# A third Strassen level in two more pairs of steps, index operations spread over six places, and a 26th buffer

## The chip, the cores and the metric

The kernel runs on one core of a Trainium2 chip. A core has five engines that run side by side, each in its own order: TensorE multiplies matrices (PE in the profile; its weight loads are PEld), VectorE (DVE), ScalarE (ACT) and GpSimd (POOL) work element by element, and SyncE (SP) here only issues DMA transfers. ScalarE and GpSimd issue transfers too. The metric is device time in microseconds (us); lower is better. Before the change it is 2588.83 us, the median of three runs (2587.49 to 2589.33).

## The reference, cut to what matters

```python
# x: (32, 128, 2048) float32; two layers, each x + ffn(cond(x))
def layer0(x):
    att = softmax(mlp(cond_128))                                  # (32, 8)
    agg_w = einsum('bk,koi->boi', att, weight)                    # a 128x128 matrix per batch
    y = einsum('boi,bih->boh', agg_w, x) + (att @ bias_k)[:, :, None]
    out = einsum('bsd,od->bso', y, W) + bias                      # 2048 x 2048
    xa = einsum('bsd,erd->ebsr', y, A)                            # 16 low-rank terms
    return x + out + einsum('ebsr,eor,e->bso', xa, Bf, coeffs * scales)

def layer1(x):
    y = grouped_conv_9_taps(x) + (cond_128 @ c_weight.T)[:, :, None] + fside
    t = y.reshape(4096, 2048)[:, perm].reshape(4096, 16, 128)
    t = gelu(einsum('bhd,hdm->bhm', t, up))                       # 16 heads, 128 -> 512
    t = einsum('bhm,hmd->bhd', t, down).reshape(4096, 2048)
    return x + t[:, argsort(perm)].reshape(32, 128, 2048)
```

The product with W is 4096 x 2048 x 2048, and it is the part that the change touches. The kernel folds the low-rank terms into W, multiplies x by that sum first, and applies the 128x128 mixing of each batch afterwards.

## The kernel before, in words

**The large product.** It is done by Strassen's method in Winograd's form, where seven products of halves take the place of eight. At the first level the seven products are the rounds P1, P2, P6, P7, P5, P3, P4 (`ROUNDS`). Each round has eight steps, g = 0 to 7; a step takes four batches, 512 rows of x. Step numbers below are these g, with the round's name; step i of the whole is 8 times the round's place plus g. Inside a step the second level is written out: `multiply` makes seven products, each of four matmuls of 128x512 into one PSUM bank, and VectorE (`add`) or, where the target is fresh, ScalarE adds or copies the bank into the accumulator in SBUF. The profile records two rows for each matmul instruction of the program, so four matmuls stand there as x8.

**The third level.** `PAIRS` names the pairs of neighbouring steps that use it: pair n is the steps 2n and 2n+1. In such a pair both steps go through `multiply_third`, which makes only the five products P1, P5, P6, P3, P7. The products P2 and P4 of both steps are together made as seven quarter products in the second step of the pair (`quarter`): each is four matmuls of 128x256, and one VectorE addition takes its bank into the accumulator. In the first round these stand after the step's five products, in P2 between them (`early`). The quarter products need three kinds of sums:
- the weights' quarters, once a round (`third_weights`): eight GpSimd subtractions of 128x256 (L393, L394, L399) and four VectorE subtractions (`quarter_ops`, L1130) in the gaps of the step;
- the x quarters, once a pair (`third_inputs`): four additions or subtractions of 128x512 (L419 to L422) from the x tiles of both steps, on the engine that the caller gives, put into a tile named `sq`;
- the accumulator of the first step, which is held until the second has ended (`held`); both are then stored.

**What runs beside it.** For each step GpSimd makes four sums of x (`x_combine`, L311 to L314), one step ahead. In the first round TensorE also makes the blocks of W with their low-rank terms (`w_make_two`, L223, at the top of steps 0 to 5); VectorE adds them to the loaded W (L226) and sums their rows (L243, L1140, L1141), and GpSimd stores them (L168). In P2 GpSimd forms the blocks of the next round (`outer_weights`, L283 with tile `wo_P`). Between the products VectorE makes the mixing matrices of the batches (`mixed_kernel`, L563, L565). Small preparations come from a generator, `small()`: `next(chain)` runs one piece of it at the end of a step, and from step i = 5 on two pieces. Its last piece computes the row numbers of the gathers and scatters of layer 1 on VectorE (L997 to L1005): thirteen operations on 128x16 integers.

**What sets the order.** The order of instructions on each engine is the order in which the program issues them (`manual_schedule`); the framework only adds semaphore waits. An engine works strictly in order, and a DMA queue issues strictly in order. SBUF tiles of 8 KB per partition come from one pool, `big`, with `SLOTS` buffers; a new tile takes over a buffer that was freed and waits for its last users. Eight PSUM banks go round.

**Layer 1** follows after the last round: mixing, convolution (`conv_begin`, `conv_middle`, `conv_end`, with three small tiles cq, cs, cr), then a gather, two matmuls with gelu between, and a scatter for each of 128 pairs of row group and head.

Of the kernel before, what the change touches and what calls it, by code (L numbers as in the profile page):

```python
# [8 lines left out]
FP = mybir.dt.float32  # L9
# [7 lines left out]
P = 128  # L17
B = 32
L = 2048
QW = 512  # L20
# [4 lines left out]
NPH = 4  # L25
# [6 lines left out]
GB = 4  # L32
NG = B // GB
GT = GB * P
SLOTS = 25

# [10 lines left out]


PAIRS = {
    "P1": (2, 3), "P2": (0, 1, 2), "P6": (0, 1, 2, 3), "P7": (0, 1, 2, 3),
    "P5": (0, 1, 2, 3), "P3": (0, 1, 2, 3), "P4": (0,),
}
ENDS = ("P1", "P4")
# [3 lines left out]
def adaln_ffn_kernel(  # L59
# [16 lines left out]
    nc = tc.nc  # L76

    dram = ctx.enter_context(tc.tile_pool(name="dram", bufs=1, space=DRAM))
    const = ctx.enter_context(tc.tile_pool(name="const", bufs=1))
    agp = ctx.enter_context(tc.tile_pool(name="agp", bufs=2))  # L80
    big = ctx.enter_context(tc.tile_pool(name="big", bufs=SLOTS))
    psum = ctx.enter_context(tc.tile_pool(name="psum", bufs=1, space=PSUM))
    banks = [psum.tile([P, QW], FP, name=f"bank{i}", tag=f"bank{i}") for i in range(8)]

    def slot(name, shape=(P, L)):
        return big.tile(list(shape), FP, name=name, tag="s")


    def bank():
        return banks.pop(0)  # L90

    def done(*ps):
        banks.extend(ps)
# [22 lines left out]
        for g in range(NG)  # L116
    }

    ident = const.tile([B, B], FP, name="ident", tag="ident")
    make_identity(nc, ident)  # L120
    mix = const.tile([P, KEXP, P], FP, name="mix", tag="mix")
    att_bc = const.tile([P, B * KEXP], FP, name="att_bc", tag="att_bc")
    aggb = const.tile([P, B], FP, name="aggb", tag="aggb")
# [6 lines left out]
    cs = const.tile([P, 4], FP, name="cs", tag="cs")  # L130
# [154 lines left out]
    def x_loads(r, g):  # L285
        return {
            "P1": lambda: [x_load(g, 0, 0)],
            "P2": lambda: [x_load(g, 0, 1)],
            "P6": lambda: [x_load(g, 1, 0), x_load(g, 1, 1), x_load(g, 0, 0)],
            "P7": lambda: [x_load(g, 0, 0), x_load(g, 1, 0)],  # L290
            "P5": lambda: [x_load(g, 1, 0), x_load(g, 1, 1)],
            "P4": lambda: [x_load(g, 1, 1)],
            "P3": lambda: [x_load(g, 0, 1), part_load("s2", g)],
        }[r]()

    def x_combine(r, g, ts):

        a = ts[0]
        tt = nc.gpsimd.tensor_tensor
        if r == "P6":  # L300

            b, a, c = ts
            pieces(b, b, a, ALU.add)
            pieces(a, b, c, ALU.subtract)
            part_store("s2", g, a)
        if r in ("P7", "P5", "P3"):
            pieces(a, a, ts[1], ALU.add if r == "P5" else ALU.subtract)
        xa[steps.index((r, g))] = a
        s = slot(f"s_{r}{g}", (P, 4, QW))
        a11, a12, a21, a22 = a[:, 0, 0], a[:, 1, 0], a[:, 0, 1], a[:, 1, 1]  # L310
        tt(s[:, 0], a21, a22, ALU.add)  # L311
        tt(s[:, 1], s[:, 0], a11, ALU.subtract)
        tt(s[:, 2], a11, a21, ALU.subtract)
        tt(s[:, 3], a12, s[:, 1], ALU.subtract)  # L314
        return {
            "P1": a11, "P2": a12, "P3": s[:, 3], "P4": a22,
            "P5": s[:, 0], "P6": s[:, 1], "P7": s[:, 2],
        }
# [90 lines left out]
    def in_pair(r, g):  # L409
        return g // 2 in PAIRS[r]  # L410

    def third_inputs(i, eng):

        (x11, x12), (x21, x22) = (
            [xa[n][:, 1, :, h * NQ : (h + 1) * NQ] for h in range(2)] for n in (i, i + 1)
        )
        tt = eng.tensor_tensor
        t = slot(f"sq_{i}", (P, 4, 2, NQ))
        tt(t[:, 0], x21, x22, ALU.add)  # L419
        tt(t[:, 1], t[:, 0], x11, ALU.subtract)  # L420
        tt(t[:, 2], x11, x21, ALU.subtract)
        tt(t[:, 3], x12, t[:, 1], ALU.subtract)  # L422
        return {
            "P1": x11, "P2": x12, "P3": t[:, 3], "P4": x22,
            "P5": t[:, 0], "P6": t[:, 1], "P7": t[:, 2],
        }
# [126 lines left out]
    late, ins, pms, xgs, x1ts, va, vb, hts, open_ = {}, {}, {}, {}, {}, {}, {}, {}, {}  # L553
# [135 lines left out]
    def conv_product(ps, k, i, v, first, last):  # L689

        for r, (out, rhs) in enumerate(zip(halves(ps), halves(v))):
            w = late["tw"][:, k - 1] if 1 <= k <= 4 else late["te"][:, k // 5]
            nc.tensor.matmul(  # L693
                out, lhsT=w[:, 2 * i + r], rhs=rhs,
                start=first and r == 0, stop=last and r == 1, skip_group_check=True,
            )

    def biased(out, ps, c, i, bias, scale):

        for r in range(2):  # L700
            for j in range(2):
                part = slice((2 * r + j) * NM, (2 * r + j + 1) * NM)
                b = 2 * c + j
                nc.scalar.activation(
                    out[:, part], ps[:, part], AF.Identity,
                    bias=bias[:, 2 * i + r, b : b + 1], scale=scale,
                )

    def conv_tile(c, i, name):
        return agp.tile([P, QW], FP, name=f"{name}_{c}{i}", tag=name, bufs=1)  # L710

    def conv_begin(c, i):
        px, py = bank(), bank()
        v = va[c, i]
        conv_product(px, 1, i, v[:, 0], True, False)
        conv_product(py, 3, i, v[:, 2], True, False)
        q, s = conv_tile(c, i, "cq"), conv_tile(c, i, "cs")
        biased(q, px, c, i, ctxb, 2.0)
        nc.scalar.mul(s, py, 2.0)
        open_[c, i] = px, py, q, s  # L720

    def conv_middle(c, i):
        px, py, q, s = open_[c, i]
        v = va[c, i]
        conv_product(px, 2, i, v[:, 1], False, False)
        conv_product(py, 4, i, v[:, 3], False, True)
        r = conv_tile(c, i, "cr")
        biased(r, py, c, i, ctxb, 2.0)
        nc.vector.tensor_tensor(q, q, px, ALU.subtract)
        nc.vector.tensor_tensor(s, s, py, ALU.subtract)  # L730

        nc.vector.tensor_tensor(v[:, 2], px, r, ALU.add)
        done(py)
        open_[c, i] = px, q, s, r
# [39 lines left out]
    def stage_second(c, n):  # L774
        if n in (6, 9):
            conv_middle(c, int(n == 9))
        if n in (5, 8):
            conv_inputs(c, int(n == 8), 1)
        if n in (0, 2):
            mix_begin(2 * c + n // 2)  # L780
# [5 lines left out]
    def third_products(c, n):  # L786
        if n in (5, 8):
            conv_begin(c, int(n == 8))
        if n in (6, 9):
            conv_end(c, int(n == 9))  # L790
        if n in (0, 2):
            mix_work(2 * c + n // 2)
# [71 lines left out]
        ws.append(t)  # L864

    def late_loads():
        late["tw"] = slot("tw_l", (P, 4, GR, P))
        nc.sync.dma_start(late["tw"].rearrange("p k r c -> p (k r c)"), tw_d)
        late["w1"] = slot("w1", (P, NPH, QW))
        nc.sync.dma_start(late["w1"].rearrange("p f n -> p (f n)"), w1_d.to_broadcast([P, L]))  # L870
        late["fb"] = slot("fb", (P, NPH, QW))
        nc.sync.dma_start(
            late["fb"].rearrange("p f n -> p (f n)"), fbias.to_broadcast([P, L])
        )


    def small():
# [3 lines left out]
        def take(rows, cols):  # L881
            used[0] += cols
            return sm[0:rows, used[0] - cols : used[0]]
# [8 lines left out]
        adiag = take(B, B * KEXP)  # L892
        ones = take(P, P)
        nc.gpsimd.memset(ones, 1.0)
        yield

        p0 = bank()
# [55 lines left out]
        for o in range(NPH):  # L953
# [44 lines left out]
        nc.vector.tensor_scalar(  # L998
            orow[:, 0], pos, 0x1FC, None, ALU.bitwise_and
        )  # L1000
        nc.vector.tensor_scalar(orow[:, 1], pos, 9, None, ALU.logical_shift_right)
        nc.vector.tensor_tensor(row, row, orow[:, 0], ALU.add)
        nc.vector.tensor_tensor(row, row, orow[:, 1], ALU.add)
        for g in range(NG):
            nc.vector.tensor_scalar(orow[:, g], pos, g * L, None, ALU.add)  # L1005
        yield


    ctx.enter_context(tc.manual_schedule())
# [44 lines left out]
    unsummed, unsummed_first = [], list(first)  # L1054
    olds = {}
    chain = small()
    nxt, waiting, ts, quarter_ops = {}, {}, {}, []
    heads = [(g, h) for g in range(NG) for h in range(NH)]
# [5 lines left out]
    for i, (r, g) in enumerate(steps):  # L1064
        ri = i // NG
        last_round = ri + 1 == len(ROUNDS)
        if i + 1 < len(steps):
            if i + 1 not in xs:
                xs[i + 1] = x_loads(*steps[i + 1])
            if not last_round:  # L1070
                lhs[i + 1] = x_combine(*steps[i + 1], xs.pop(i + 1))
                if g == 2 * PAIRS[r][0]:
                    quarters, quarter_ops = third_weights(r, rhs)
                if in_pair(r, g) and g % 2 == 0 and g > 0 and r != "P6":
                    sq = third_inputs(i, nc.gpsimd)
        if i == 0:
            olds_load(0)
        if i + 1 < len(steps) and not last_round and i != NG - 1:
# [31 lines left out]
        if last_round and g == 0:  # L1110
            quarters, quarter_ops = third_weights(r, rhs)
            late_loads()
# [49 lines left out]
        if in_pair(r, g) and g % 2 == 0 and (g == 0 or r == "P6" or last_round):  # L1162
            sq = third_inputs(i, nc.gpsimd if r in ENDS else nc.vector)
# [97 lines left out]
```

## Time and profile before

| what | value |
|---|---|
| median of three runs | 2588.83 us (2587.49 to 2589.33) |
| the profiled execution, its own time | 2590.78 us |
| its span (first to last instruction) | 2589.0 us |
| TensorE busy | 2574.6 us, 99% of the span |
| VectorE busy | 1514.5 us, 58% |
| GpSimd busy | 1362.8 us, 53% |
| ScalarE busy | 532.2 us, 21% |
| DMA, mean | 235 GB/s |
| mean granted TensorE clock | 0.999 |

The profile of one execution has a page with the busy time of each engine, its share in slices of the span, the DMA queues and the costliest groups of instructions. The trace behind it answers narrower questions: the waits (which instruction of an engine waited for which of another, total us, times, longest), the timeline (instructions in order of time: start, duration, engine, line, operation, output<-input, shape, count, and in brackets the idle time before it and what ended it), and the busy time by windows. Matmuls overlap, so a row's duration is longer than the distance to the next row; the distances of the starts are what they cost. Busy time says little about an engine that is not the last one waited for.

### The profile page before, as it was taken

To read this page: it belongs to the slowest core of one execution; us is meant where nothing else is said; L and a number is where in the kernel's file an instruction comes from. 1 tells how busy PE (TensorE), PEld (TensorE's weight loads), DVE (VectorE), ACT (ScalarE), POOL (GpSimd) and SP (SyncE) were. 2 spreads that over 40 slices of the span, in tenths; PEclk is the share of its full clock that TensorE was granted. 3 is DMA by queue.
4 is the path that set the end of the run, shared out by engine and by line. 5 is a ranking of instruction groups with operands and counts; after the bars stand their busy time and mean duration, and the time that the engine had idled before them with its cause. 6 is when DMAs were issued, how large, how long until landed. Compare 5 with 4: busy or idle time off the path is not lost. (4 is left out here: it accounts for less than half of the span.)

```text
span 2589.0 us, 21703 instructions
## 1 busy us (share of the span) xinstructions
PE 2574.6 (99%) x6998; PEld 1328.4 (51%) x6998; DVE 1514.5 (58%) x2368; ACT 532.2 (21%) x1099; POOL 1362.8 (53%) x1124
## 2 busy tenths in 40 slices
PE   9999999999999999999999999999999999999999
PEld 4445554455555555555554454455544454455543
DVE  5656565466555676654377666667666666666601
ACT  0000000000000000000011244444444444444432
POOL 7323756988977845977514234343444334434222
PEclk9999999999999999999999999999999999999999
DMA  7543467778467477573766887777767877787432
GB/s 324 210 163 129 162 235 317 289 296 336 187 246 296 189 316 297 199 317 156 254 229 228 256 303 254 241 243 232 228 225 234 258 232 222 226 257 234 161 127 89
DMA packets 186577, 608.30 MB, mean 235 GB/s; under 512 B 17632, under 2 KB 91872, under 8 KB 142304
## 3 DMA queue, kind: packets, MB, share of 16 engines
q1 hardware_dynamic: 147936, 473.48, 50.8%
q0 software_dynamic: 32704, 130.04, 15.0%
q10 hardware_dynamic: 5824, 3.40, 0.4%
q8 instruction: 56, 0.92, 0.1%
q14 instruction: 57, 0.47, 0.1%
HBM read 372.45 MB, written 200.84 MB: 221 GB/s over the span
## 5 line engine op out<-in xcount | busy, mean ns | idle before, releaser
L837 PE MATMUL bank<-t,ws 128*128 128x512 f32 x1024 | 460.3, 592 | 0.0
L848 PE MATMUL bank<-gl,ws 128*128 128x512 f32 x1024 | 460.2, 592 | 0.0
L855 POOL DMA_INDIRECT out<-t,orow x128 | 152.1, 1188 | 538.8 <-DVE t L853 478.6
L840 ACT ACTIVATE gl<-bank 128x512 f32<-128x512 f32 x512 | 305.8, 598 | 418.0 <-PE bank L837 415.4
L447 PE MATMUL bank<-P_t,s_P 128*128 128x512 f32 x704 | 314.5, 595 | 3.0 <-DVE p L440 3.0
L848 PEld LDWEIGHTS bank<-gl,ws 128*128 128x128 f32 x1024 | 194.6, 190 | 233.0 <-issue 231.5
L837 PEld LDWEIGHTS bank<-t,ws 128*128 128x128 f32 x1024 | 194.6, 190 | 226.6 <-issue 222.7
L586 POOL TENSOR_TENSOR x<-x,fb 128x512 f32<-128x512 f32 x128 | 177.1, 1412 | 227.5 <-DMA x<-in_x 159.5
L853 DVE TENSOR_TENSOR t<-bank,t 128x512 f32<-128x512 f32 x128 | 88.4, 690 | 325.0 <-PE bank L848 325.0
L440 DVE TENSOR_TENSOR u<-bank,u 128x512 f32<-128x512 f32 x204 | 134.0, 687 | 233.1 <-PE bank L447 214.1
L592 ACT ACTIVATE bank<-w,aggb 128x512 f32<-128x512 f32 x128 | 80.8, 684 | 867.3 <-DMA w<-w_d 855.0
L447 PE MATMUL bank<-wo_P,s_P 128*128 128x512 f32 x544 | 241.6, 592 | 0.0
L283 POOL TENSOR_TENSOR xt<-xt,xt 128x512 f32<-128x512 f32 x128 | 163.1, 1307 | 107.4 <-DMA xt<-in_xT 89.4
L447 PEld LDWEIGHTS bank<-P_t,s_P 128*128 128x128 f32 x704 | 134.3, 191 | 156.6 <-issue 152.7
L311 POOL TENSOR_TENSOR s_P<-xt 128x512 f32<-128x512 f32 x56 | 73.9, 1319 | 212.4 <-DMA xt<-in_xT 170.5
L565 DVE SCALAR_TENSOR_TENSOR ags<-mix,att_bc,ags 128x128 f32<-128x128 f32 x224 | 181.3, 810 | 4.7
L447 PEld LDWEIGHTS bank<-wo_P,s_P 128*128 128x128 f32 x544 | 103.4, 190 | 116.5 <-issue 113.6
L821 POOL DMA_INDIRECT t<-hx_d,row x128 | 131.2, 1025 | 57.0 <-issue 23.2
L440 DVE TENSOR_TENSOR p<-bank,p 128x512 f32<-128x512 f32 x84 | 56.6, 688 | 116.3 <-PE bank L447 111.6
L693 PE MATMUL bank<-va,tw_l 128*128 128x256 f32 x512 | 122.0, 380 | 2.2 <-DVE va L677 2.2
L447 PE MATMUL bank<-wo_P,xt 128*128 128x512 f32 x272 | 122.3, 592 | 0.0
L460 PE MATMUL bank<-P_q,sq 128*128 128x256 f32 x528 | 120.7, 379 | 0.4 <-DVE u L468 0.4
(191 smaller groups left out, 3515.8 us busy)
## 6 DMA issues: line engine op xcount, KB each, us to landing
xt<-in_xT SPq DMA_DIRECT2D x88, 1024.0 KB, 10.6
u<-u_d SPq DMA_DIRECT2D x40, 1024.0 KB, 10.2
wo_P<-wb_d SPq DMA_DIRECT2D x36, 1024.0 KB, 13.0
u<-c_d SPq DMA_DIRECT2D x64, 512.0 KB, 7.3
x<-in_x SPq DMA_DIRECT2D x32, 1024.0 KB, 9.3
xg<-x SPq DMA_DIRECT2D x256, 128.0 KB, 5.4
hx_d<-x1t SPq DMA_DIRECT2D x32, 1024.0 KB, 6.7
hx_d<-ht SPq DMA_DIRECT2D x32, 1024.0 KB, 4.8
```

The costliest lines, as they stand in the source:

```text
L283: nc.gpsimd.tensor_tensor(out[:, i, j], a[:, i, j], b[:, i, j], op)
L440: nc.vector.tensor_tensor(to, ps, to, ALU.add)
L447: nc.tensor.matmul(ps, lhsT=lhs[k][:, bass.ts(kc, P)], rhs=rhs[k][kc], start=first and kc == 0, stop=last and kc == 3, skip_group_check=True,)
L460: nc.tensor.matmul(out, lhsT=sq[k][:, i, bass.ts(kc, P)], rhs=quarters[i][k][kc], start=first and i == 0 and kc == 0, stop=last and i == 1 ...
L565: nc.vector.scalar_tensor_tensor(ag, mix[:, k], att, ag, ALU.mult, ALU.add)
L586: nc.gpsimd.tensor_tensor(xt[:, f], xt[:, f], late["fb"][:, f], ALU.add)
L693: nc.tensor.matmul(out, lhsT=w[:, 2 * i + r], rhs=rhs, start=first and r == 0, stop=last and r == 1, skip_group_check=True,)
L821: nc.gpsimd.indirect_dma_start(out=t.rearrange("p k t -> p (k t)"), out_offset=None, in_=hx_d[g].rearrange("l k t -> l (k t)"), in_offset= ...
L837: nc.tensor.matmul(pu, lhsT=w[:, m * P : (m + 1) * P], rhs=t[:, 0], start=True, stop=True)
L840: nc.scalar.activation(gl[m], pu, AF.Gelu)
L848: nc.tensor.matmul(pd, lhsT=w[:, (MC + m) * P : (MC + m + 1) * P], rhs=gl[m], start=(m == 0), stop=(m == MC - 1),)
L855: nc.gpsimd.indirect_dma_start(out=out, out_offset=bass.IndirectOffsetOnAxis(ap=orow[:, g, h : h + 1], axis=0), in_=t[:, 1], in_offset=None,)
```

## The change

Five edits:
- `PAIRS`: in P1 pair 1 (steps 2 and 3) and in P2 pair 3 (steps 6 and 7) now use the third level. The weights' quarters of P1 are therefore made at step 2 instead of step 4.
- The x quarters of P2's steps 6 and 7 are made on VectorE, at the top of step 6. Those of the other pairs stay where they were.
- The last piece of `small()` is cut by `yield` so that its thirteen index operations come out in six pieces.
- `SLOTS` goes from 25 to 26. The three convolution tiles, which had a pool of their own, become parts of one buffer taken from `big` at the start of the last round.
- The 32x32 identity is made in a part of the `small` tile, in the generator's first piece, instead of at the start of the kernel in a tile of its own.

```diff
-SLOTS = 25
+SLOTS = 26
...
 PAIRS = {
-    "P1": (2, 3), "P2": (0, 1, 2), "P6": (0, 1, 2, 3), "P7": (0, 1, 2, 3),
+    "P1": (1, 2, 3), "P2": (0, 1, 2, 3), "P6": (0, 1, 2, 3), "P7": (0, 1, 2, 3),
     "P5": (0, 1, 2, 3), "P3": (0, 1, 2, 3), "P4": (0,),
 }
...
-    ident = const.tile([B, B], FP, name="ident", tag="ident")
-    make_identity(nc, ident)
...
-    def conv_tile(c, i, name):
-        return agp.tile([P, QW], FP, name=f"{name}_{c}{i}", tag=name, bufs=1)
+    def conv_tile(n):
+        return late["cv"][:, n]
...
-        q, s = conv_tile(c, i, "cq"), conv_tile(c, i, "cs")
+        q, s = conv_tile(0), conv_tile(1)
...
-        r = conv_tile(c, i, "cr")
+        r = conv_tile(2)
...
     def late_loads():
+        late["cv"] = slot("cv", (P, NPH, QW))
...
         nc.gpsimd.memset(ones, 1.0)
+        ident = take(B, B)
+        make_identity(nc, ident)
         yield
...
         nc.vector.tensor_scalar(
             orow[:, 0], pos, 0x1FC, None, ALU.bitwise_and
         )
+        yield
         nc.vector.tensor_scalar(orow[:, 1], pos, 9, None, ALU.logical_shift_right)
         nc.vector.tensor_tensor(row, row, orow[:, 0], ALU.add)
+        yield
         nc.vector.tensor_tensor(row, row, orow[:, 1], ALU.add)
         for g in range(NG):
             nc.vector.tensor_scalar(orow[:, g], pos, g * L, None, ALU.add)
-        yield
+            if g % 2 == 1:
+                yield
...
                 if in_pair(r, g) and g % 2 == 0 and g > 0 and r != "P6":
-                    sq = third_inputs(i, nc.gpsimd)
+                    sq = third_inputs(i, nc.vector if r == "P2" and g == NG - 2 else nc.gpsimd)
```

## The prediction

> **What bounds the kernel now.** I read the busy times first, then the waits of TensorE, then the timeline at its one long wait.
>
> ```profile
> PE 2574.6 (99%) x6998; PEld 1328.4 (51%) x6998; DVE 1514.5 (58%) x2368; ACT 532.2 (21%) x1099; POOL 1362.8 (53%) x1124
> ...
> PE bank L447 <- DVE p L440: 3.0, 1, 3.0
> PE bank L693 <- DVE va L677: 2.2, 4, 0.9
> ```
>
> TensorE works for 2574.6 of 2589.0 us. Its waits add up to 8.1 us, and one wait is 3.0 of them. So only two things can shorten the kernel: fewer matmul cycles, and that one wait. Anything put on another engine is free until TensorE waits for it. The wait lies at P2's step 4 (TensorE's rows, then VectorE's, by start and duration):
>
> ```profile
> 390.68 3.60 PE L447 MATMUL bank<-w,xt 128*128 128x512 f32 x8
> 394.11 3.60 PE L447 MATMUL bank<-P_t,s_P 128*128 128x512 f32 x8
> 400.67 5.37 PE L447 MATMUL bank<-P_t,s_P 128*128 128x512 f32 x8 [2.97 <-DVE p L440]
> 405.88 7.03 PE L447 MATMUL bank<-w,s_P 128*128 128x512 f32 x16
> ...
> 390.88 1.29 DVE L440 TENSOR_TENSOR p<-bank,p 128x512 f32<-128x512 f32 x2 [1.83 <-PE bank L447]
> 392.08 1.22 DVE L997 TENSOR_SCALAR row<-pos 128x16 int32<-128x16 int32 x1
> ...
> 396.99 1.19 DVE L1003 CUSTOM_DVE_ANT_0 row<-row,orow 128x32 uint16<-128x32 uint16 x1
> 398.10 1.83 DVE L1005 TENSOR_SCALAR orow<-pos 128x16 int32<-128x16 int32 x8
> 399.85 0.68 DVE L440 TENSOR_TENSOR p<-bank,p 128x512 f32<-128x512 f32 x1
> ...
> 389.53 9.83 POOL L283 TENSOR_TENSOR wo_P<-wo_P,wo_P 128x512 f32<-128x512 f32 x8
> ```
>
> The thirteen index operations stand on VectorE between the last additions of step 3 and the first of step 4. Five of them take 1.2 to 1.3 us each while GpSimd computes (389.5 to 399.4); the eight of L1005, most of which run after GpSimd is done, take 1.83 together. P6 continues in P1's bank, so TensorE waits for the addition of 399.85. What it loses is more than 2.97: four matmuls are 3.43 apart, so step 4's fourth product would have begun at 394.11 + 6.87 = 400.98; it began at 405.88. **4.90 us** are lost: the wait, and a granted clock of 0.64 and 0.80 in the two 3 us windows from 400.0 on.
>
> **The change, part by part.**
>
> *Third level, two more pairs.* The starts of P2's products give the price. Steps 4 and 5 would serve but for the wait, so I take steps 2 and 3 (paired) and 6 (not):
>
> ```profile
> 344.25 3.60 PE L447 MATMUL bank<-w,xt 128*128 128x512 f32 x8
> 390.68 3.60 PE L447 MATMUL bank<-w,xt 128*128 128x512 f32 x8
> 442.00 7.03 PE L349 MATMUL bank<-w,xt 128*128 128x512 f32 x16
> 466.03 7.03 PE L349 MATMUL bank<-w,xt 128*128 128x512 f32 x16
> ```
>
> The pair before 344.25 began at 297.83: 46.42 for two steps, against 2 x 24.03 = 48.06. By instructions: 16 matmuls of 128x512 at 0.858 go (13.73), 28 of 128x256 at 0.432 come (12.09). That is **1.64 us a pair, 3.28 for both**, all of it on TensorE's path. It is certain as long as the operands are ready.
>
> *First round, what feeds steps 2 and 3.* GpSimd's eight weight quarters move two steps forward and four x quarters are new; at steps 4 and 5 the same twelve took from 191.46 to 205.24, 13.8 us. GpSimd's queue then holds back the stores of two W blocks. The longest chain goes through them: x of step 3 lands at 114.1 as before, its sums end at 119.1, the twelve at 132.9, the stores are issued by 134.0 and land 6.1 later (median of that row) at 140.1; x of step 4 takes the buffer they free and lands some 10.6 later, 150.7; sums and two stores to 156.8, landing 162.9; then the second W block of step 4 is loaded into that buffer, 11.0: 173.9. VectorE first needs it at about 180.5. Hidden, with 6.6 us to spare.
> VectorE's new work is also beside TensorE, but it decides when w_make's banks come free. In step 2 it has, after the addition of P3 (131.75 to 132.4), a weight quarter, two row sums, P7's addition and L1140, L1141; the like sequence of step 4 reached P7's end +1.0, and L1140/L1141 add 1.9: first W addition at 138.0, TensorE 0.8 later (399.85 to 400.67) at 138.8, where it wants 138.56. Cost 0.2; 1.2 if the row sums stretch as at 193.79 (3.41 for 2.48). At step 4 the last quarter's addition now comes after L1141, but ScalarE's table load (1.28, at 178.93 before) no longer stands between the softmax pieces, since the last copy before it comes earlier: W additions from 179.9, TensorE at 180.7 for a wanted 180.1, 0.6 lost against 0.4 before. Cost 0.2; 0 to 1.6 if the table load stays late.
>
> *Index operations.* In the program's order two now stand before step 4 of P2, five before step 5, four before step 6, two before step 7. Step 4: 2.5 us, the addition ends at about 395.3 in the old scale for a P6 at 397.55: **the 4.90 go**. Step 5: all five can meet GpSimd's `wo_P` sums (row above, 1.2 to 1.3 each), 6.3 us. In the new scale the step begins at 406.2; VectorE is through its additions at 407.7, the five end at 414.0, the addition, L563 and L565 (0.35 to 1.37) follow, and the first quarter's addition begins at 415.3 to 416.7. Its bank is wanted again at 416.5, after P1, two quarters and P5. Cost 0 to 1.0, taken 0.5.
>
> *x quarters on VectorE.* They stand at the top of step 6 (435.5 in the new scale), behind four index operations, ahead of the addition that P6 waits for at 442.35. Rows of the same operations: 0.68 (L1130) without GpSimd, 1.04 to 1.21 (L419 to L422) beside it. GpSimd is idle then:
>
> ```profile
> 427.31 9.93 POOL L283 TENSOR_TENSOR wo_P<-wo_P,wo_P 128x512 f32<-128x512 f32 x8
> 437.53 0.57 POOL L546 DMA_DIRECT2D t_d<-wo_P  x1 [0.30 <-POOL wo_P L283]
> 456.07 9.93 POOL L283 TENSOR_TENSOR xt<-xt,xt 128x512 f32<-128x512 f32 x8 [17.97 <-PE bank L349]
> ```
>
> So: additions to 436.9, four index operations 0.6, four quarters 2.5, TensorE could go on at 440.8. Cost 0, spare 1.6 us. If GpSimd were busy throughout: 4 x 1.25 + 4 x 1.1 put it at 447.1, 4.8 lost. Even if GpSimd stayed at its old times it would be done at 437.2. The x tile of step 7 is issued by 401 and landed long before.
> The Trainium skill ("GPSIMD Engine Reference", Specifications) says that GpSimd shares SBUF interfaces with VectorE and contends with Vector instructions that have two SBUF inputs. It speaks against this move, since a quarter has two. By it alone the move could cost the 4.8; the idle row at 437.5 makes it 0.
>
> *26 buffers, convolution tile, identity.* The new tiles take the added buffer in rounds one and two; in the last round 25 are left, as before. SP's order changes in places where a store is put off to the pair's end. Bounds: nothing, or the two waits of 0.5 and 0.4 that later rounds have (0.9 gained); TensorE waits for no load in the trace, so I take 0. GpSimd's next round (`inner_weights`) starts 6.5 earlier, TensorE's step 8.1 earlier; its first late operand keeps about 3 us. Identity: 0.3 us on GpSimd, idle for 20 us then.
>
> **Sum.** -3.28 - 4.90 + 0.2 + 0.2 + 0.5 = **-7.3 us** against the profiled execution's 2590.78, so 2583.5 in its scale. That execution is 1.95 above the median; on the median, 2588.83 - 7.3 = **2581.5**.
>
> The Trainium skill ("TensorE: Matmul & The Clock Gate", What's actually happening) puts the half clock after an idle window of about 3.4 us. Here 2.97 us of idling already cost clock. By the page the wait would be worth 2.97 and the sum -5.4; the rows say 4.90.
>
> **Rivals.**
> - *The wait moves instead of going.* Step 5's five index operations hold the quarter's bank for 3 us or more and the clock falls again: 4.9 come back, -3.3 + 0.4, **2586.0**. For it: the pile is only halved. Against: it needs the additions 2 us later than my worst row. 0.10.
> - *VectorE blocks step 6.* GpSimd runs late and meets the quarters: +4.8 and, like the row at 400.67, 1.9 of clock: about **2588.2**, no change. Needs GpSimd some 5 us later than before. 0.09.
> - *The first round stalls (slower).* The chain of stores and loads above feeds a W block late at step 4. With 6.6 us of cover it starts to cost beyond 173.9 + 6.6, and outweighs -7.3 by more than 0.2% once it is 6.6 + 7.3 + 5.2 = 19 us late. Two landings at twice their medians make 17 to 22: about **2595**. Against: DMA moves 46 to 275 GB/s between 140 and 200. 0.07.
> - *The change does less than it says*: an operand of a quarter is late in both pairs and the 3.28 go. 4.9 remain, **2584.8**. 0.03.
>
> **How the numbers follow.** My forecast has 0.71. A measurement tells 0.2%, 5.2 us, from no change: the border is 2583.65. Faster: 0.71 and a little of the rest, 0.73; same: 0.10 + 0.09 + part, 0.20; slower 0.07. The range: from all costs nothing and the 0.9 gained, -9.1 or 2579.7, and 0.2 for the runs' spread, to the first rival, 2586.0. Only the second and third rivals lie outside.
>
> **What the profile will show.** P2's steps 6 and 7 in 46.4 us and P1's 2 and 3 likewise; no wait at P2's step 4 and no clock below 1.00 there; L419 to L422 on VectorE at P2's step 6 at about 0.7; L1001 to L1005 at 1.2 to 1.3 at step 5. I am wrong if TensorE waits over 2 us anywhere between 100 and 500.

## The result, and the profile after

The changed kernel takes 2604.97 us, the median of six runs (2601.39 to 2606.92). In the same series the kernel before takes 2588.51 us (six runs, 2586.43 to 2589.58). The ratio is 1.0064, with a 95% interval from 1.0054 to 1.0073: the change costs 16.5 us, where 7.3 were expected to be gained.

The profiled execution of the changed kernel took 2604.03 us, with a span of 2602.2. The spans of the two profiled executions differ by 13.2 us; the rest up to 16.5 is that one of them lies 2.3 above its median and the other 0.9 below it. The view to read first is the waits of TensorE (which instruction waited for which, total us, times, longest):

```profile
PE bank L445 <- DVE p L438: 8.4, 1, 8.4
PE bank L458 <- DVE u L466: 3.3, 1, 3.3
PE bank L221 <- DVE w L224: 3.1, 2, 2.8
```

The change makes the line numbers ahead of `late_loads` smaller by two: L445 here is L447 of before, L458 is L460, L221 and L224 are L223 and L226, L281 is L283, and L309 to L312 and L417 to L420 are the sums of x and the x quarters. Behind it they are larger: L933 here is L932 of before, L1003 to L1008 are L1001 to L1005, and L1134 is L1130. The wait of 3.0 us of before is gone and three new ones stand in its place. In the timeline of the changed kernel, TensorE's rows:

```profile
208.03 3.70 PE L221 MATMUL bank<-bf_sb,a_sb 128*128 128x512 f32 x8
214.53 7.11 PE L221 MATMUL bank<-tb,sa 128*128 128x512 f32 x12 [2.81 <-DVE w L224]
224.92 2.31 PE L445 MATMUL bank<-w,xt 128*128 128x512 f32 x5
...
394.32 3.60 PE L445 MATMUL bank<-w,xt 128*128 128x512 f32 x8
397.76 7.03 PE L445 MATMUL bank<-P_t,s_P 128*128 128x512 f32 x16
404.62 7.03 PE L445 MATMUL bank<-w,s_P 128*128 128x512 f32 x16
...
440.75 3.60 PE L445 MATMUL bank<-w,xt 128*128 128x512 f32 x8
487.17 3.17 PE L445 MATMUL bank<-wo_P,xt 128*128 128x512 f32 x7
506.07 10.03 PE L445 MATMUL bank<-wo_P,s_P 128*128 128x512 f32 x16 [8.45 <-DVE p L438]
515.93 0.59 PE L445 MATMUL bank<-wo_P,xt 128*128 128x512 f32 x1
...
890.84 1.03 PE L458 MATMUL bank<-wo_P,xt 128*128 128x256 f32 x4
901.20 4.00 PE L458 MATMUL bank<-P_q,sq 128*128 128x256 f32 x10 [3.31 <-DVE u L466]
921.82 3.60 PE L445 MATMUL bank<-wo_P,xt 128*128 128x512 f32 x8
```

The rows of before that answer to six of these:

```profile
208.79 3.70 PE L223 MATMUL bank<-bf_sb,a_sb 128*128 128x512 f32 x8
221.27 1.02 PE L447 MATMUL bank<-w,xt 128*128 128x512 f32 x2
...
490.07 3.60 PE L447 MATMUL bank<-wo_P,xt 128*128 128x512 f32 x8
507.23 3.60 PE L447 MATMUL bank<-wo_P,xt 128*128 128x512 f32 x8
...
882.02 1.03 PE L460 MATMUL bank<-wo_P,xt 128*128 128x256 f32 x4
908.48 3.60 PE L447 MATMUL bank<-wo_P,xt 128*128 128x512 f32 x8
```

Read the differences of the starts, after minus before. Ahead of P1's step 5 the changed kernel leads by 0.76 us; after the wait near 211 it is 3.65 behind. So the wait costs **4.4 us**, more than its 2.8 of idling, since the granted clock falls after it (0.76 from 214.5 to 221.5). The wait at P2's step 4 is gone: 394.32, 397.76 and 404.62 stand at the regular 3.43 and 6.87. P2's last pair takes 487.17 - 440.75 = 46.42 us. At the start of P6 the lead is 2.90 (490.07 before), and at step 1 of P6 the kernel is 8.70 behind (515.93 against 507.23): **11.6 us** for the wait of 8.4. Near 895 the lag goes from 8.82 to 13.34, **4.5 us**. The three together are 20.5, and 13.2 - 20.5 = -7.3 us: outside the three waits the kernel gained about the sum of the prediction. All of it is there by the start of P6: 0.76 ahead of P1's step 5, 4.90 at P2's step 4, 1.64 in P2's last pair.

What stands in front of each wait shows in the rows of the other engines in the changed kernel (VectorE's and GpSimd's, near 211, near 497 and near 895):

```profile
208.91 4.97 DVE L933 SCALAR_TENSOR_TENSOR aggb<-att_bc,small,aggb 128x32 f32<-128x32 f32 x7
207.56 1.27 POOL L309 TENSOR_TENSOR s_P<-xt 128x512 f32<-128x512 f32 x1 [8.01 <-PE bank L445]
...
494.88 9.81 POOL L281 TENSOR_TENSOR xt<-xt,xt 128x512 f32<-128x512 f32 x8
504.73 0.69 DVE L1134 TENSOR_TENSOR P_q<-P_t 128x512 f32<-128x512 f32 x1 [13.23 <-POOL xt L281]
505.34 0.68 DVE L438 TENSOR_TENSOR p<-bank,p 128x512 f32<-128x512 f32 x1
...
890.01 1.11 DVE L417 TENSOR_TENSOR sq<-xt 128x512 f32<-128x512 f32 x1
891.16 1.64 DVE L418 TENSOR_TENSOR sq<-sq,xt 128x512 f32<-128x512 f32 x1
892.72 1.75 DVE L419 TENSOR_TENSOR sq<-xt,xt 128x512 f32<-128x512 f32 x1
894.39 1.75 DVE L420 TENSOR_TENSOR sq<-xt,sq 128x512 f32<-128x512 f32 x1
886.85 5.40 POOL L281 TENSOR_TENSOR xt<-xt,xt 128x512 f32<-128x512 f32 x4
892.32 1.60 POOL L309 TENSOR_TENSOR s_P<-xt 128x512 f32<-128x512 f32 x1
```

The same operations in before, near 211 and near 885:

```profile
209.83 2.09 DVE L932 SCALAR_TENSOR_TENSOR aggb<-att_bc,small,aggb 128x32 f32<-128x32 f32 x7
219.80 1.27 POOL L311 TENSOR_TENSOR s_P<-xt 128x512 f32<-128x512 f32 x1 [13.47 <-PE bank L223]
...
881.20 0.87 DVE L419 TENSOR_TENSOR sq<-xt 128x512 f32<-128x512 f32 x1
882.10 1.10 DVE L420 TENSOR_TENSOR sq<-sq,xt 128x512 f32<-128x512 f32 x1
883.12 1.21 DVE L421 TENSOR_TENSOR sq<-xt,xt 128x512 f32<-128x512 f32 x1
884.25 1.21 DVE L422 TENSOR_TENSOR sq<-xt,sq 128x512 f32<-128x512 f32 x1
884.87 1.17 POOL L399 TENSOR_TENSOR P_q<-wo_P,wo_P 128x256 f32<-128x256 f32 x1
```

- *Near 211.* Seven small bias operations take 4.97 us while GpSimd makes the sums of x of step 6. In before they took 2.09, and those sums began at 219.80. The additions for the new weight (L224) are queued behind them.
- *Near 497.* The first VectorE weight quarter of P6 waits 13.23 us for GpSimd's sum of x tiles of the next step. The two have no data in common. By the program, the quarter tile has taken over the buffer of an x tile that this sum is the last to read; e5 below tests it. TensorE waits for the addition of 505.34, queued behind.
- *Near 895.* VectorE's four x quarters of P5's first pair take 6.3 us beside GpSimd's 128x512 operations. In before they took 4.4 (0.87, 1.10, 1.21, 1.21), beside GpSimd's 128x256 operations. The next small operation behind them (L561, 128x128) takes 1.31 against 0.27 and adds 1.0 to the lateness.

### The profile page after: what moved, and what is told of

The parts are those of the page before. It is cut to its first block, busy times and chain, and to the rows that moved or that the text cites. A ratio compares the mean times of both kernels' runs of the same rounds, so it can differ in the third digit from the quotient of the medians.

```text
span 2602.2 us, 21822 instructions
## 1 busy us (share of the span) xinstructions
PE 2577.1 (99%) x7046; PEld 1340.0 (51%) x7046; DVE 1521.1 (58%) x2382; ACT 532.2 (20%) x1099; POOL 1365.7 (52%) x1128
## 5 line engine op out<-in xcount | busy, mean ns | idle before, releaser
L445 PE MATMUL bank<-P_t,s_P 128*128 128x512 f32 x768 | 340.8, 592 | 0.0
L445 PE MATMUL bank<-wo_P,s_P 128*128 128x512 f32 x544 | 244.6, 598 | 8.4 <-DVE p L438 8.4
L445 PEld LDWEIGHTS bank<-P_t,s_P 128*128 128x128 f32 x768 | 145.9, 190 | 166.6 <-issue 162.2
L281 POOL TENSOR_TENSOR xt<-xt,xt 128x512 f32<-128x512 f32 x128 | 164.4, 1317 | 123.2 <-DMA xt<-in_xT 123.2
L309 POOL TENSOR_TENSOR s_P<-xt 128x512 f32<-128x512 f32 x56 | 74.9, 1337 | 195.1 <-DMA xt<-in_xT 146.7
L445 PEld LDWEIGHTS bank<-wo_P,s_P 128*128 128x128 f32 x544 | 104.4, 192 | 127.1 <-issue 114.7
L438 DVE TENSOR_TENSOR p<-bank,p 128x512 f32<-128x512 f32 x96 | 64.7, 688 | 130.3 <-PE bank L445 128.5
L458 PE MATMUL bank<-P_q,sq 128*128 128x256 f32 x576 | 133.3, 383 | 3.3 <-DVE u L466 3.3
L458 PEld LDWEIGHTS bank<-P_q,sq 128*128 128x128 f32 x576 | 110.4, 192 | 36.2 <-issue 22.0
## 6 DMA issues: line engine op xcount, KB each, us to landing
u<-u_d SPq DMA_DIRECT2D x40, 1024.0 KB, 10.3
```

The source lines that it names most:

```text
L281: nc.gpsimd.tensor_tensor(out[:, i, j], a[:, i, j], b[:, i, j], op)
L438: nc.vector.tensor_tensor(to, ps, to, ALU.add)
L445: nc.tensor.matmul(ps, lhsT=lhs[k][:, bass.ts(kc, P)], rhs=rhs[k][kc], start=first and kc == 0, stop=last and kc == 3, skip_group_check=True,)
L458: nc.tensor.matmul(out, lhsT=sq[k][:, i, bass.ts(kc, P)], rhs=quarters[i][k][kc], start=first and i == 0 and kc == 0, stop=last and i == 1 ...
```

## The experiments

The theory after the first look: the added buffers of the third level and the 26th buffer make the three waits, not the edits that the prediction priced. Twelve kernels were timed, in three series, each with the kernel before on the same chip (its medians 2588.39, 2588.51 and 2587.84). The change itself was timed in the series above, so the column to compare is the difference from before:

| kernel | median us | against before of its series | ratio, 95% interval |
|---|---|---|---|
| the change | 2604.97 | +16.5 | 1.0064 [1.0054, 1.0073] |
| e1: index operations alone | 2584.1 | -4.3 | 0.9985 [0.9976, 0.9994] |
| e2: 26 buffers alone | 2598.75 | +10.4 | 1.0040 [1.0026, 1.0053] |
| e3: change without P2's pair | 2593.54 | +5.2 | 1.0017 [1.0008, 1.0026] |
| e5: change, P6's quarter tile in another buffer | 2594.62 | +6.2 | 1.0027 [1.0016, 1.0038] |
| e6: change, bias operations later | 2599.82 | +11.3 | 1.0036 [1.0022, 1.0049] |
| e8: change, P5's x quarters on GpSimd | 2599.0 | +10.5 | 1.0040 [1.0026, 1.0053] |
| e10: e1 and P1's pair, 25 buffers | 2590.69 | +2.2 | 1.0006 [0.9997, 1.0015] |
| e13: e10 and P2's pair, P6's tiles mended | 2591.8 | +3.3 | 1.0015 [1.0006, 1.0024] |
| e9: change, all three waits mended | 2583.64 | -4.2 | 0.9983 [0.9974, 0.9992] |
| e12: change with 25 buffers | 2602.9 | +15.1 | 1.0057 [1.0043, 1.0071] |
| e14: e9, P2's x quarters on GpSimd | 2584.95 | -2.9 | 0.9988 [0.9979, 0.9997] |
| e15: e9 without P1's pair | 2584.99 | -2.9 | 0.9988 [0.9979, 0.9997] |

### Parts alone

e1 is the kernel before with this one edit:

```diff
             orow[:, 0], pos, 0x1FC, None, ALU.bitwise_and
         )
+        yield
...
+        yield
...
         for g in range(NG):
             nc.vector.tensor_scalar(orow[:, g], pos, g * L, None, ALU.add)
-        yield
+            if g % 2 == 1:
+                yield
```

> The kernel before with one part of the change alone: the index operations spread over six places. The theory (the sum of the prediction came out where nothing new waits, and three new waits of TensorE are what made the kernel slower): the wait at step 4 of P2 goes with its half clock, 4.9 us, so 2588.5 - 4.9 = 2583.6 us, and no wait of TensorE over 2 us is left between 100 and 500 us. The rival (the wait at that place is only passed on, to step 5 or to a later one): 2588 us.

Measured: 2584.1 us, -4.3, and no wait of TensorE over 1.5 us. The wait was not passed on. No other kernel here beats it by more than the runs can tell.

e2 is the kernel before with `SLOTS = 26`, the convolution tiles in a buffer and the identity in the small tile; `PAIRS` and the index operations are those of before.

> The kernel before with the 26 buffers alone (the convolution's tiles in a buffer, the identity in the tile of small parameters; third level and index operations as before). Theory: the wait of 8.4 us at the start of P6 came from the three more buffers that the last pair of P2 holds, so it is absent here, and the wait of 3.3 us near 895 with it; the first one, near 211, came from the order in which the buffers come round (the sums of x of step 6 get the buffer that step 4's sums held, and start when step 4 ends, beside VectorE's sums of the bias), so it is here: 2588.5 + 4.4 = 2592.9 us. Rival: all three waits come from 26 buffers instead of 25: 2588.5 + 4.4 + 11.6 + 4.5 = 2609 us. Third possibility, none of them does: 2588.5 us.

Measured: 2598.75 us, +10.4. Its waits, beside the 2.9 at step 4 of P2 that before has too:

```profile
PE bank L458 <- DVE u L466: 3.3, 1, 3.3
PE bank L221 <- DVE w L224: 3.2, 2, 2.9
PE bank L445 <- DVE p L438: 2.9, 1, 2.9
```

Two of the three new waits are here without any third level added, the one at P6 is not. The theory had the wait near 895 as a consequence of the one at P6 (TensorE late, GpSimd not); that fell. The 26th buffer makes it, with what goes along with it here: the places of the convolution tiles and of the identity, which no run took apart.

e3 takes P2's last pair out of the changed kernel.

```diff
-    "P1": (1, 2, 3), "P2": (0, 1, 2, 3), "P6": (0, 1, 2, 3), "P7": (0, 1, 2, 3),
+    "P1": (1, 2, 3), "P2": (0, 1, 2), "P6": (0, 1, 2, 3), "P7": (0, 1, 2, 3),
```

> The changed kernel without the third level in P2's last pair. Theory: P6's second quarter tile finds a buffer that is free, the wait at the start of P6 goes (11.6 us with its half clock), and the one near 895 goes with it (4.5 us), because GpSimd is no longer 9 us ahead of TensorE there; the wait near 211 stays. 2605.0 - 11.6 - 4.5 + 1.6 = 2590.5 us by the changed kernel; by the kernel before 2588.5 - 4.9 - 1.6 + 4.4 = 2586.4 us; I take 2588 us. Rival (the waits come from 26 buffers): 2606.6 us.

Measured: 2593.54 us. The wait at P6 is gone; those of 2.8 near 211 and 3.3 near 890 stay. So the wait at P6 belongs to P2's pair, and again the wait near 895 does not need it. The expected 2588 was too low by about what that wait costs.

### The wait at the start of P6

e5 is the changed kernel with another order of first uses at step 0 of P6 (step i = 16), and so other buffers for four tiles. `olds_load` loads the accumulators of earlier rounds to which a step adds.

```diff
...
+                q1 = None
+                if i == 2 * NG:
+                    olds_load(i + 1)
+                    q1 = slot(f"{r}_q1", (P, 4, 2, NQ))
+                    nc.vector.tensor_tensor(
+                        q1[:, 0], rhs["t4"][:, 0:2, NQ:QW], rhs["t4"][:, 0:2, 0:NQ], ALU.subtract
+                    )
                 lhs[i + 1] = x_combine(*steps[i + 1], xs.pop(i + 1))
                 if g == 2 * PAIRS[r][0]:
-                    quarters, quarter_ops = third_weights(r, rhs)
+                    quarters, quarter_ops = third_weights(r, rhs, q1)
...
```

> The changed kernel with the same work, in which only the order of the first uses of four tiles at the start of P6 is another, so that the second quarter tile gets a buffer that TensorE left at the end of step 15, and the first quarter tile (GpSimd's own) the buffer that GpSimd's sums of x free. Theory: the wait of 8.4 us goes (11.6 with its half clock), and the one near 895 with it, since it is a consequence (GpSimd 9 us further ahead of TensorE): 2605.0 - 16.1 = 2588.9 us. Rival (the wait near 895 has a cause of its own): 2593.4 us. Rival (the wait at P6 comes from somewhere else than the buffer): 2605 us.

Measured: 2594.62 us, 10.3 less than the change. The wait of 8.4 is gone with the same work done, so it came from the buffer. In its place TensorE waits 2.2 us for GpSimd's weight quarters. The wait near 895 is unchanged:

```profile
PE bank L221 <- DVE w L224: 3.4, 3, 2.8
PE bank L458 <- DVE u L466: 3.3, 1, 3.3
PE bank L458 <- POOL P_q L392: 2.2, 2, 1.4
```

Why P2's last pair brings this on, as read from the program: it keeps P2's two quarter tiles and one more `sq` tile in use to the end of step 7, three buffers that steps 6 and 7 did not hold before, and step 6's accumulator with them; the change adds one buffer. P6's second quarter tile then gets one that comes free 17 us into its own step (487.17 to 504.69).

### The two waits of the 26th buffer

e6 is the changed kernel with the bias operations one step later.

```diff
         done(p3)
+        yield
         ab = att_bc.rearrange("p (b k) -> p b k", k=KEXP)
...
-
-        yield
         for r in range(GR):
```

> The changed kernel, in which the eight bias operations of VectorE (aggb, 128x32) stand one step later, after step 5, where no making of a weight follows them. Theory (the wait of 2.8 us near 211 is VectorE being slowed in these operations by GpSimd's sums of x of step 6, with weight additions queued behind): the wait goes with its half clock, 4.4 us: 2605.0 - 4.4 = 2600.6 us. The other two waits stay as they are. Rival (the additions are late for another reason): 2605 us.

Measured: 2599.82 us, 5.2 less than the change. TensorE no longer waits near 211, and at their new place, at 249.7, the seven operations take 2.09 us again.

e8 is the changed kernel with the x quarters of P5's first pair on GpSimd.

```diff
-            sq = third_inputs(i, nc.gpsimd if r in ENDS else nc.vector)
+            sq = third_inputs(i, nc.gpsimd if r in ENDS + ("P5",) else nc.vector)
```

> The changed kernel, in which the x quarters of P5's first pair are made by GpSimd and not by VectorE. Theory (with 26 buffers GpSimd runs some 7 us further ahead of TensorE there, so that VectorE's four operations fall on GpSimd's 128x512 operations and take 6.3 us, not 4.4; the wait of 3.3 us near 895 is that): the wait goes with its half clock, 2605.0 - 4.5 = 2600.5 us, and no new wait on GpSimd, which is ahead by more than the 5 us that it now works longer. Rival (GpSimd has no time for them, so TensorE waits for the x quarters or for the x of step 34): 2605 us or more.

Measured: 2599.0 us, 6.0 less than the change, and no wait near 895. GpSimd had the time: the quarters run there from 884.92 to 889.99, and TensorE needs them at 895.84.

That GpSimd is further ahead with 26 buffers shows in its own waits. Before, its rows ahead of P5:

```profile
842.80 1.27 POOL L253 TENSOR_TENSOR P_t<-wo_P,P_t 128x512 f32<-128x512 f32 x1 [2.23 <-PE bank L447]
849.69 1.27 POOL L254 TENSOR_TENSOR P_t<-wo_P,P_t 128x512 f32<-128x512 f32 x1 [5.62 <-PE bank L447]
```

and in the changed kernel there is one, shorter:

```profile
851.62 1.27 POOL L252 TENSOR_TENSOR P_t<-wo_P,P_t 128x512 f32<-128x512 f32 x1 [0.66 <-PE bank L445]
```

Before, GpSimd waits 7.85 us for two of the new round's weight tiles, until TensorE has left their buffers; with one buffer more it waits 0.66. This goes with the count of buffers, and not with the third level: e1, e10 and e12 with 25 have both waits (2.0 to 2.2 and 5.62), e2 and e3 with 26 have only one, of 0.92 and 0.94. From there on its queue has no gap up to the x quarters, so all of it moves forward. It begins its next sums of x tiles (L283, L281) 5.5 us after VectorE's first x quarter in before (886.70 against 881.20), and 3.2 us ahead of it in the change (886.85 against 890.01).

### The pairs with 25 buffers

e10 is e1 with P1's pair, e13 is e10 with P2's pair (its x quarters on VectorE, as in the change) and with P6's quarter tiles both made by VectorE and first written ahead of the sums of x, so that they take the buffers which step 7 of P2 leaves.

```diff
...
+                if i == 2 * NG:
+                    quarters, quarter_ops = third_weights(r, rhs, True)
                 lhs[i + 1] = x_combine(*steps[i + 1], xs.pop(i + 1))
-                if g == 2 * PAIRS[r][0]:
+                if g == 2 * PAIRS[r][0] and i != 2 * NG:
                     quarters, quarter_ops = third_weights(r, rhs)
...
```

> The kernel before with the index operations in six places and the third level in P1's steps 2 and 3, with 25 buffers. Theory (this pair costs nothing in the buffers, and the wait near 211 comes from the 26th buffer): 2584.1 - 1.6 = 2582.5 us, no wait over 2 us. Rival (the pair itself makes the wait near 211 or another, by its three more buffers or by 5 us more on GpSimd): 2584.1 - 1.6 + 4.4 = 2586.9 us or more.

> All of the change but the 26th buffer (25 buffers, convolution tiles and identity as before), and at the start of P6 the second and first quarter tiles of the weights are first written ahead of the sums of x, by VectorE, so that they get the buffers that step 15 leaves, and VectorE makes both of them. Theory (the cause of the wait at P6 is the buffer, of the other two the 26th buffer): 2584.1 - 2 x 1.6 = 2580.8 us, no wait over 2 us. Rival (a new wait at step 17, for the olds' load, which now waits for the sums of x, or for the x quarters): 2584 to 2588 us.

Measured: 2590.69 and 2591.8 us. Neither has the waits near 211 and 895, as the theory said. But both have another one, at the making of the weights in step 3 of P1, so the rival of e10 was right on the pair: it does make a wait by its buffers. In e10, VectorE's and SyncE's rows:

```profile
145.24 2.48 DVE L226 TENSOR_TENSOR w<-bank,w 128x512 f32<-128x512 f32 x4 [5.73 <-DMA w<-in_WT]
...
111.94 28.58 SPq L164 DMA_DIRECT2D w<-in_WT  x2
```

With 25 buffers a load of W waits 28.6 us for its buffer, and TensorE waits 5.3 us for the additions. In the changed kernel the same two loads take 4.32 us of SyncE's queue, and the additions wait for nothing. So P1's pair needs the 26th buffer as long as the order of the first uses stays; another order there was not run. In e13 the wait at P6 is gone, and one of 2.0 us at P6's step 1 stands there, for VectorE's additions.

e12 is the whole change but for the 26th buffer.

> The change without the 26th buffer and what makes room for it: the index operations in six places, both pairs, P2's last x quarters on VectorE, 25 buffers. Theory: the wait of 5.3 us near 146 (P1's pair with 25 buffers) and the one at the start of P6 (P2's last pair) are both here, the ones near 211 and 895 are not: 2590.7 - 1.6 + 11.6 = 2600.7 us, so that the 26th buffer alone, in the change, costs 2605.0 - 2600.7 = 4.3 us. Rival (without it the two pairs take buffers from each other and it is far worse): above 2605 us.

Measured: 2602.9 us, with the two waits that were expected (5.4 near 145 and 9.2 at P6). In the change, then, the 26th buffer is worth about nothing (+16.5 with it, +15.1 without): it takes away one wait and makes two others.

### All three waits taken away

e9 is the changed kernel with the edits of e6 and e8, and P6's quarter tiles as in e13, with the load of the olds ahead of them as in e5.

> The whole change with all three waits taken away: the bias operations one step later, P5's first x quarters on GpSimd, and P6's quarter tiles first written ahead of the sums of x and made by VectorE. Theory (the three waits are all that the change lost, and the sum of the prediction, -7.3, is what it gains without them): 2588.5 - 7.3 = 2581.2 us; by the experiments, 2605.0 - 5.1 - 6.0 - 11.6 = 2582.3 us; up to 3 us more if VectorE's longer work at the start of P6 makes TensorE wait there, as it did for 2.0 us in the version with 25 buffers. Rival (something else was lost too): 2588 us or more.

Measured: 2583.64 us, 4.2 less than before, where the change was 16.5 more: 20.7 us regained. Its longest wait (L467 and L475 are L458 and L466 of the change):

```profile
PE bank L467 <- DVE p L475: 2.1, 1, 2.1
```

So the three waits, 20.5 by the starts, were what the change lost. But the gain is that of e1 (4.2 against 4.3), although e9 has both pairs. The profiles show where theirs goes: e9 is 2.19 us ahead of e1 at the start of P6 (482.73 against 484.92) and 0.17 behind at the start of its step 2 (531.51 against 531.34). The wait of 2.1 us at 512, in step 1 of P6, lies between. VectorE is late there by its x quarters, which begin 1.2 us late, for GpSimd's sum of x tiles, and take 6.0 us beside GpSimd's sums of x. No version without this wait was run.

e14 and e15 take one part each out of e9: the x quarters of P2's last pair go back to GpSimd, and P1's pair is left out.

> The version without the three waits, but with the x quarters of P2's last pair made by GpSimd, as in the other pairs. Theory (GpSimd is the engine that is late at the change from P2 to P6, and 5 us more there come out as a wait of TensorE or in VectorE's late operations at step 17): 2581.2 + 3 to 5 = 2584 to 2586 us. Rival (GpSimd has the time): 2581 us.

> The version without the three waits, but without the third level in P1's steps 2 and 3. Theory (that pair gives its 1.6 us of TensorE's time and nothing else once no wait follows): 2581.2 + 1.6 = 2582.8 us. Rival (the pair gives nothing, or loses): 2581 us or less.

Measured: 2584.95 and 2584.99 us. Both medians lie 1.3 us above that of e9, but the intervals of the three overlap, and the profiles do not put the two alike. Without P1's pair (e15) TensorE begins the two matmuls with gelu of layer 1 0.9 us later than in e9 (1462.88 against 1461.97), near the 1.2 that the pair left in the change. With the x quarters on GpSimd (e14) it begins them at the same 1461.97: GpSimd's 5 us more cost nothing up to there, as the rival said. The 1.3 us between these two executions arise behind that point, most of them at 1467, where TensorE waits 0.7 us for VectorE in e14 alone. The edit does not touch that part, and why the wait is there stays open.

## Why the prediction was wrong

It said -7.3 us and a kernel that is faster at 0.73; the kernel is 16.5 us slower. Step by step:

- *What bounds the kernel: TensorE, and its one wait.* Right for the kernel before. It was read as if the list of waits were the list of places that can wait. The waits of a kernel without slack appear where there were none.
- *Third level, 1.64 a pair.* Right: 46.42 for P2's steps 6 and 7, as forecast. The matmul rows of P1's pair are the same in kind; with the 0.4 for VectorE's lateness it left 1.2, and the profile has 60.56 (before) - 59.33 (after) = 1.2 from the start of step 2 to the W blocks made at step 4.
- *Index operations, -4.90.* Right, mechanism and size: the starts show no gap at step 4; TensorE gains 4.90 there (from 3.64 behind at 394.32 to 1.26 ahead at 411.49), and e1 alone measures -4.3. The 0.5 at step 5 were too much; 0.33 us lost ahead of P1's step 2 (118.15 against 117.82), which the sum did not have, nearly make up for it, so that the sum comes out to a tenth is in part luck. Of the five operations at step 5 forecast at 1.2 to 1.3 the first took 0.99 and the others less than 0.2 each, since GpSimd's sums of x ended at 413.86:

```profile
412.90 0.99 DVE L1003 TENSOR_SCALAR orow<-pos 128x16 int32<-128x16 int32 x1
413.81 0.16 DVE L1004 CUSTOM_DVE_ANT_0 row<-row,orow 128x32 uint16<-128x32 uint16 x1
414.00 0.17 DVE L1006 CUSTOM_DVE_ANT_0 row<-row,orow 128x32 uint16<-128x32 uint16 x1
414.10 0.29 DVE L1008 TENSOR_SCALAR orow<-pos 128x16 int32<-128x16 int32 x2
```

- *x quarters on VectorE at P2's step 6, 0.* Right: 0.69, 0.69, 0.69 and 0.68 us from 442.46 on, no wait, and by e14 the move makes no difference to TensorE up to the matmuls with gelu of layer 1.
- *26 buffers, "nothing, or ... 0.9 gained; TensorE waits for no load in the trace, so I take 0".* **This step failed, and with it the forecast.** Its bounds held no loss at all. The 26th buffer alone costs 10.4 us (e2), and in the change the two waits that it makes cost 4.4 and 4.5. Loads of TensorE were the wrong thing to look at: the buffers decide when GpSimd may start, and GpSimd's start decides how fast VectorE is. The two waits of GpSimd on TensorE (2.23 and 5.62) were in the trace of before; at P5 they kept GpSimd's 128x512 operations behind VectorE's x quarters.
- *"The new tiles take the added buffer in rounds one and two."* Wrong in the count. P2's last pair alone needs three buffers beyond what steps 6 and 7 had, with one added. At P6 the prediction looked at when GpSimd starts ("its first late operand keeps about 3 us") and not at which buffer P6's own tiles get. That is the 11.6 us.
- *First round, hidden with 6.6 us to spare.* Right in the changed kernel that it is hidden. It hung on the 26th buffer, which the text priced at nothing: without it the load of a W block is 5.7 us late for VectorE, at step 3 and not at step 4 (e10).
- *The rivals.* The third rival had the right sign at 0.07, with another place and mechanism (stores and loads of the first round, at step 4). "The wait moves" and "VectorE blocks step 6" did not occur. "I am wrong if TensorE waits over 2 us anywhere between 100 and 500" was the right test; 2.81 at 211 and 8.45 from 497.6 to 506.1 met it.

The Trainium skill ("GPSIMD Engine Reference", Specifications) says that GpSimd shares SBUF interfaces with VectorE and contends with Vector instructions that have two SBUF inputs. The trace agrees, at two places for which the prediction did not ask: 4.97 us against 2.09 for the same seven operations, and 6.3 against 4.4 for the same four. The prediction weighed the sentence at the one place where the change moves an operation; it holds as well wherever the change moves GpSimd in time.

## What to carry to other kernels

A change in the number or use of buffers is a change in the schedule of every engine that waits for one: go through the tiles that are first written after it, look up which buffer each gets and who leaves that last, and give the step a price with a loss in it. An idle time of a helper engine that seems to cost nothing can be what keeps two engines from slowing each other; when it goes, ask on whom the engine's work falls next. And where a change bundles a cure for a measured wait with edits that are to buy little, measure the cure alone: here it has the whole gain.

## What the runs showed of the hardware

The clock after a wait is not decided by the wait's length alone. The windows of the changed kernel and of e3 around the same wait (from:to, length, busy us of PE, PEld, DVE, ACT and POOL, then the granted clock, DMA share, GB/s), 3.31 and 3.34 us long:

```profile
897.00:907.00 10.00, 6.69 (x21) 4.75 (x20) 9.57 (x14) 0.00 (x0) 9.84 (x9) 0.83 0.00 1
```

```profile
887.00:897.00 10.00, 6.66 (x24) 4.29 (x23) 9.93 (x15) 0.00 (x0) 9.84 (x9) 1.00 0.00 1
```

One lost clock and the other did not; with the same wait of 3.34 and 3.35 us, e5 and e6 went down to 0.66 over the like 10 us. The wait of 2.81 us at 211 lost it (0.83 from 208.5 to 218.5), the one of 2.09 in e9 did not (1.00 from 510 to 520). The Trainium skill ("TensorE: Matmul & The Clock Gate", What's actually happening) says that the activity window is free-running and about 3.4 us long, and that the half clock comes after at least one idle window. That the same wait can come out either way agrees with a free-running window; that 2.81 us sufficed does not agree with a whole idle one. What else decides it is open. For reading runs it means that nearly the same wait can cost 2.9 us more in one execution than in another: behind it, the eight quarter matmuls that waited take 3.53 us in e3 (890.96 to 894.49) and 6.39 in e6 (896.35 to 902.74).

In these rows a small operation suffers more, for its size, from a busy neighbour: the same 128x32 operation on VectorE took 0.27 us alone and up to 1.31 beside GpSimd's 128x512 sums, where the x quarters of 128x512 went from 0.69 (P2's step 6) to 1.97 at most (e5 and e9).
